# Turning softmax rows into columns: through DRAM and 32×32 blocks on VectorE in place of TensorE transposes

## The chip, the cores and the metric

The kernel runs on one core of a Trainium2 chip. The metric is the device time in microseconds (us) of one execution. Engines are named as the profile names them: PE (TensorE; PEld is its weight load), DVE (VectorE), ACT (ScalarE), POOL (GpSimd) and SP (SyncE, which here only issues DMAs). Every execution works on the same inputs.

## The reference

A graph convolution on 1250 nodes of 1024 features is followed by a transformer layer over the same 1250 tokens. Only the layer's attention is touched by the change. It has 16 heads of width 64, and its value and output projections are mixtures of 8 experts with a gate of two.

```python
q = _rope(jnp.einsum('bsd,hdp->bhsp', x, Wq))
k = _rope(jnp.einsum('bsd,hdp->bhsp', x, Wk))
gv = _gate(x, Wsel_v)                 # sigmoid, the two largest of 8 kept
v = jnp.einsum('bsd,bhse,hedp->bhsp', x, gv, Wv)
att = jax.nn.softmax(jnp.einsum('bhsp,bhtp->bhst', q, k) / np.sqrt(P), axis=-1)
o = jnp.einsum('bhst,bhtp->bhsp', att, v)
go = _gate(x, Wsel_o)
return jnp.einsum('bhsp,bhse,hepd->bsd', o, go, Wo)
```

All of it is float32. Ahead of it stand a layer norm, the graph convolution and another layer norm; behind it a residual with layer norms and a feed-forward block.

## The kernel before

**Arithmetic.** A float32 operand is split into a rounded part `hi` and the rest `lo`, both of a type that PE multiplies at full rate. `dot` makes three matmuls of each product: hi·hi, hi·lo and lo·hi. ACT makes `hi` (a copy that rounds), and DVE or POOL makes `lo` (a subtraction).

**Stages.** (1) The graph convolution, in tiles of KT = 125 nodes. (2) `queries_keys`: for each head, queries and keys together (128 rows: 64 of queries, 64 of keys) over the 1250 tokens in three pieces of columns, with the gates' work between them. (3) `values` and `attention`, interleaved. (4) `outputs`, with the last of the attention. (5) `feed_forward`.

**Stage 2.** A head's hi and lo parts are collected in the tiles `qk_hi` and `qk_lo` (two buffers each, so a head waits until the tiles of the head before the last one are free). When the head's third piece is done, SP issues six writes to DRAM (`kq_d`, lines 594 and 596): two of the key rows and four of the query rows, each of 64 rows of 1250 floats. The weights of later heads (line 123) are loaded by the same SP queue.

**Stage 3.** `values` makes, for each head and tile of 125 tokens, a product of eight steps of depth with 512 columns (8 experts × 64), in four value steps of six matmuls each; then DVE multiplies by the gate (`ve`, line 717) and adds the experts (`v`, line 720). There are 40 value steps a head and 640 in all.

`attention` works on chunks of 256 query rows, five a head and 80 in all, each in two halves of 128 rows. `softmax` (line 622) loads q and, once a head, k by POOL's queue; PE makes the scores in three PSUM banks (line 634); DVE takes the rows' maximum (`most`, line 637); ACT makes the exponentials and their sums (line 642); DVE multiplies the rows by 1/sum (line 647). Then the rows have to become columns, since PE sums over partitions. `split` (line 650) does that for two tiles of 125 keys at a time, five times a chunk: four transposes by PE (line 655) into a PSUM bank, `att_hi` by ACT (line 657), `att_lo` by DVE (line 659). `product` (line 664) multiplies them with the values, four matmuls of 256 columns, into the bank `po`. After the last tile the sum goes to `o_d` in DRAM by SP.

**Order.** PE's instructions stand in the order in which the program writes them (`manual_schedule`). In stage 3 this is a fixed interleaving of generators: of eight value steps seven are followed by one event of the attention, in the order of this line:

```python
for event in (0, "k", "k", 1, "k", "k", "k"):
```

0 and 1 are the halves' scores of the next chunk, and a "k" is one `split` and one `product` that was split two events earlier. The order of the other engines and of the queues is set by a scheduler when the program is built. Each engine, and SP, works through its own order and waits where it must: a later instruction does not pass an earlier one.

**Stage 4.** `outputs` takes for every pair of heads and half of the experts five column blocks of 250 tokens. SP loads `oc` (the attention's result, line 736) and `gb` (the gate, spread over partitions, line 741); DVE multiplies them (line 745); ACT and DVE split into `go_hi` and `go_lo` (lines 748 and 750); PE multiplies by the output weights, and DVE adds into `acc` (line 765).

**PSUM.** In stages 3 and 4 there are, of eight banks, two for values or outputs (`mm`), two for the transposes (`tr`), three for scores and one for `po`.

Of the kernel before, what the change touches and what calls it, by code (L numbers as in the profile page):

```python
# [11 lines left out]
F32 = mybir.dt.float32  # L12
# [10 lines left out]
N = 1250  # L23
# [13 lines left out]
CUT = NZ * KT  # L37
# [33 lines left out]
def gnn_ffn_kernel(  # L71
# [31 lines left out]
    o_d = [dram.tile([P, N], F32, name=f"o_d{j}") for j in range(NP)]  # L103
    g_d = dram.tile([P, N], F32, name="g_d")
# [61 lines left out]
    def transposed(hi, lo, c0, y, psum_tile):  # L166

        for half in range(2):
            p = psum_tile([P, 4, KT])
            for k in range(4):  # L170
                d0 = (4 * half + k) * P
                nc.tensor.transpose(p[:, k, :], y[:, d0 : d0 + P], ident[:KT, :KT])
            to = (slice(None), slice(4 * half, 4 * half + 4), slice(c0, c0 + KT))
            nc.scalar.copy(hi[to], p)
            nc.vector.tensor_tensor(lo[to], p, hi[to].bitcast(F32), ALU.subtract)
# [8 lines left out]
    with ExitStack() as gctx:  # L184
# [16 lines left out]
        with ExitStack() as bctx:  # L201
# [3 lines left out]
            with tc.tile_pool(name="ring1t", bufs=6) as r1:  # L205
                ring += [r1] * 6

                def prepare(t):
# [10 lines left out]
                    transposed(yh, yl, 0, y[:KT], lambda shape: ps.tile(shape, F32, name="tr2", bufs=2))  # L219
# [274 lines left out]
        zT = [[zpool.tile([P, ND, CUT], F32R, name=f"zT0{k}") for k in range(2)]]  # L494
        for t in range(2, NT):
            new = sums([t])
            if t - 2 < NZ:
                transposed(zT[0][0], zT[0][1], KT * (t - 2), zs.pop(0)[:KT], side_bank)
                zs += new
# [5 lines left out]
    def z_of(t, d):  # L505

        k = t if t < NZ else t - NZ
        return [part[:, d, KT * k : KT * (k + 1)] for part in zT[t >= NZ]]

    def rest_of_z():  # L510

        for t in range(NZ, NT):
            z = raws[0].tile([P, D], F32, name="w_raw")[:KT]
            move(z, z_d[t])
            transposed(zT[1][0], zT[1][1], KT * (t - NZ), z, side_bank)
# [3 lines left out]
    def gates(wpool, tmp):  # L519
# [5 lines left out]
        wide = [KT, 2 * H, NX]  # L525
        order = first_wins[:KT, None, :].to_broadcast(wide)

        def pick(chosen, v, m):

            nc.vector.tensor_reduce(m, v, AX.X, ALU.max)  # L530
# [5 lines left out]
        for t in range(NT):  # L536
            p = side_bank([KT, 2 * P])
# [3 lines left out]
            s, a, b, c = (tmp.tile([KT, 2 * H, NX], F32, name=k) for k in ("s", "a", "b", "chosen"))  # L541
            m = tmp.tile([KT, 2 * H], F32, name="m")
# [5 lines left out]
            nc.vector.tensor_tensor(gate_v[:KT, t, :].rearrange("p (h e) -> p h e", h=H), s[:, :H, :], c[:, :H, :],  # L548
                                    ALU.mult)
            nc.vector.tensor_tensor(a[:, H:, :], s[:, H:, :], c[:, H:, :], ALU.mult)  # L550
            pg = psums[-1].tile([P, KT], F32, name="po", bufs=1)
            nc.tensor.transpose(pg, a[:, H:, :].rearrange("p h e -> p (h e)"), ident[:KT, :KT])
            nc.scalar.copy(gT[:, KT * t : KT * (t + 1)], pg)
# [4 lines left out]
    def queries_keys(tab, work):  # L558
# [9 lines left out]
        chunks = [(0, 0, CUT), (1, 0, 376), (1, 376, N - CUT - 376)]  # L568
# [3 lines left out]
        for h, k in pieces:  # L572
# [19 lines left out]
            if k == 2:  # L592
                for j, part in enumerate((hi.bitcast(F32), lo.bitcast(F32))):
                    nc.sync.dma_start(kq_d[h][HD * j : HD * (j + 1), 0, :], part[HD:])
# [13 lines left out]
    with tc.tile_pool(name="qktab", bufs=1) as tab, tc.tile_pool(name="qkwork", bufs=2) as work, \  # L608
            tc.tile_pool(name="gatet", bufs=2) as tmp:
        turns, rest = queries_keys(tab, work), rest_of_z()  # L610
        interleave(islice(turns, 2), rest, 1, 1 / 3)
        interleave(turns, gates(tab, tmp), 1, 3)

# [3 lines left out]
    def attention(pool):  # L617


        keys, made = {}, {}  # L620

        def softmax(h, c, i):
# [5 lines left out]
            q = pool.tile([P, 2, P], F32R, name="q", bufs=4)  # L628
# [9 lines left out]
            p = pool.tile([P, N], F32, name="p", bufs=5)  # L638
            parts = pool.tile([P, 3], F32, name="parts", bufs=4)
            for k, k0 in enumerate(starts):  # L640
                n = KW if k == 2 else KW - 2
                nc.scalar.activation(p[:, k0 : k0 + n], s[:, k, :n], AF.Exp, bias=most,  # L642
                                     accum_out=parts[:, k : k + 1])
            total = pool.tile([P, 1], F32, name="total", bufs=4)
            nc.vector.tensor_reduce(total, parts, AX.X, ALU.add)
            nc.vector.reciprocal(total, total)
            nc.vector.tensor_scalar_mul(p, p, total)
            made.setdefault((h, c), []).append(p)

        def split(h, c, k):  # L650

            t = side_bank([KT, 2, QW])
            for j in range(2):
                for i, p in enumerate(made[h, c]):
                    nc.tensor.transpose(t[:, j, P * i : P * (i + 1)], p[:, KT * (k + j) : KT * (k + j + 1)], ident)  # L655
            hi = pool.tile([KT, 2, QW], F32R, name="att_hi", bufs=3)
            nc.scalar.copy(hi, t)  # L657
            lo = pool.tile([KT, 2, QW], F32R, name="att_lo", bufs=3)
            nc.vector.tensor_tensor(lo, t, hi.bitcast(F32), ALU.subtract)  # L659
            return hi, lo  # L660

        sums = {}

        def product(h, c, k, parts):
            if k == 0:
                sums[h, c] = psums[-1].tile([P, QW], F32, name="po", bufs=1)
            po = sums[h, c]
            for j in range(2):
                for part in parts:
                    nc.tensor.matmul(po, lhsT=v_of[h][:, k + j, :], rhs=part[:, j, :],  # L670
                                     start=(k + j == 0 and part is parts[0]),
                                     stop=(k + j == NT - 1 and part is parts[1]))
            if k + 2 < NT:
                return
            o = pool.tile([HD, QW], F32, name="o", bufs=2)
            nc.scalar.copy(o, po[HD:])
# [250 lines left out]
```

## Time and profile before

| what | value |
|---|---|
| median of 3 runs | 3134.45 us (3130.17 to 3136.78) |
| profiled execution, its own time | 3137.92 us |
| its span, first to last instruction | 3136.1 us |
| mean granted PE clock | 0.985 |
| PE busy | 3023.9 us (96%) |
| DVE, ACT, POOL busy | 62%, 35%, 22% |
| moved by DMA | 254.86 MB, mean 81 GB/s |

| stage | from, to (us from the span's start) | PE busy in it | DMA share |
|---|---|---|---|
| queries, keys, gates | 314 to 593 | 262.43 | 0.58 |
| values and attention | 593 to 2015 | 1416.31 | 0.21 |
| outputs | 2026 to 2997 | 940.65 | 0.36 |

How it is read. Busy time is the time in which an engine has an instruction under way. Matmuls are pipelined, so the spacing of their starts, not their duration, is what one costs PE. The DMA share is the mean busy share of the core's 16 DMA engines. In the groups, what stands behind the second bar is the idle time of the engine just before the group's instructions and what ended it. A profile shows one execution; the span and the device time of that execution differ by 1.8 us, and that execution took 3.5 us more than the median.

### The profile page before, as it was taken

What the parts mean: (1) busy time and instruction counts of PE and PEld (TensorE: products, weight loads), DVE (VectorE), ACT (ScalarE), POOL (GpSimd) and SP (SyncE); (2) the same over time, 40 slices, a digit from 0 to 9 for tenths busy, and PEclk for the clock granted to TensorE, in tenths of its full rate; (3) what the DMA queues carried; (4) which work ended last, traced back from release to release, by engine and by line L of the source; (5) the groups of instructions that cost most, each with busy time, mean ns of one, the idle gap of its engine ahead of it and who ended that gap; (6) DMA issues with size and microseconds to landing.
All of it is one profiled execution on the core that took longest, in us unless ns stands there. A gap on an engine that the chain in (4) does not pass through costs nothing. (4 is left out here: it accounts for less than half of the span.)

```text
span 3136.1 us, 41143 instructions
## 1 busy us (share of the span) xinstructions
PE 3023.9 (96%) x15618; PEld 2554.4 (81%) x15618; DVE 1957.2 (62%) x3477; ACT 1098.1 (35%) x2472; POOL 702.2 (22%) x570
## 2 busy tenths in 40 slices
PE   6989899999999999999999999899999999999998
PEld 5777889888888888888888888787777777777787
DVE  7965687566666666666666666664444444444685
ACT  5762323234444444444444444431112112111222
POOL 2000334322222122222212222202112112112223
PEclk9999999999999999999999999999999999999999
DMA  3116555612221121222112122434333333333212
GB/s 111 60 41 190 167 142 160 167 43 52 54 55 37 42 52 47 54 55 53 43 39 53 46 54 54 102 94 123 106 85 98 96 85 103 90 82 109 75 41 92
DMA packets 151825, 254.86 MB, mean 81 GB/s; under 512 B 14521, under 2 KB 111801, under 8 KB 151458
## 3 DMA queue, kind: packets, MB, share of 16 engines
q1 hardware_dynamic: 103934, 210.68, 23.9%
q0 software_dynamic: 45824, 31.22, 5.2%
q10 hardware_dynamic: 1860, 10.24, 1.1%
q8 instruction: 124, 2.03, 0.3%
q14 instruction: 83, 0.68, 0.1%
HBM read 200.25 MB, written 56.96 MB: 82 GB/s over the span
## 5 line engine op out<-in xcount | busy, mean ns | idle before, releaser
L129 POOL TENSOR_TENSOR w_lo<-w_raw,w_hi 128x1024 fp32r<-128x1024 f32 x148 | 372.3, 2525 | 1078.0 <-ACT w_hi L127 1069.6
L141 PE MATMUL mm<-w_hi,go_lo 128*125 128x512 f32 x1280 | 507.6, 399 | 24.6 <-DVE go_lo L750 24.5
L139 PE MATMUL mm<-w_hi,go_hi 128*125 128x512 f32 x1280 | 509.5, 398 | 8.8 <-ACT go_hi L748 7.9
L139 PE MATMUL mm<-w_hi,zT 128*125 128x512 f32 x1280 | 508.4, 397 | 4.6 <-ACT raw L584 4.6
L140 PE MATMUL mm<-w_lo,go_hi 128*125 128x512 f32 x1280 | 509.9, 398 | 0.0
L140 PE MATMUL mm<-w_lo,zT 128*125 128x512 f32 x1280 | 507.1, 396 | 0.1
L141 PE MATMUL mm<-w_hi,zT 128*125 128x512 f32 x1280 | 507.1, 396 | 0.0
L642 ACT ACTIVATE p<-s,most 128x416 f32<-128x416 f32 (+1 forms) x480 | 286.0, 605 | 332.8 <-DVE most L637 329.2
L765 DVE TENSOR_TENSOR acc<-acc,mm 125x512 f32<-125x512 f32 x320 | 217.4, 683 | 163.1 <-PE mm L141 163.1
L659 DVE TENSOR_TENSOR att_lo<-tr,att_hi 125x512 fp32r<-125x512 f32 x400 | 262.6, 685 | 88.7 <-ACT att_hi L657 88.6
L141 PEld LDWEIGHTS mm<-w_hi,go_lo 128*125 128x125 f32 x1280 | 239.9, 187 | 93.6 <-DVE go_lo L750 33.7
L748 ACT CAST go_hi<-gb 128x500 fp32r<-128x500 f32 x160 | 98.2, 614 | 602.2 <-PE mm L140 600.6
L657 ACT CAST att_hi<-tr 125x512 fp32r<-125x512 f32 x400 | 235.1, 589 | 179.0 <-PE tr L655 176.0
L139 PEld LDWEIGHTS mm<-w_hi,go_hi 128*125 128x125 f32 x1280 | 239.9, 187 | 68.3 <-ACT go_hi L748 8.2
L745 DVE TENSOR_TENSOR gb<-gb,oc 128x500 f32<-128x500 f32 x160 | 103.8, 690 | 303.0 <-DMA gb<-g_d 301.8
L141 PEld LDWEIGHTS mm<-w_hi,zT 128*125 128x125 f32 x1280 | 238.3, 186 | 60.5
L140 PEld LDWEIGHTS mm<-w_lo,go_hi 128*125 128x125 f32 x1280 | 239.7, 187 | 58.4
L637 DVE TENSOR_REDUCE most<-s 128x1 f32<-128x1254 f32 x160 | 234.2, 1464 | 81.0 <-PE s L634 80.6
L655 PEld LDWEIGHTS tr<-ident,p 128*125 128x125 f32 x1600 | 234.9, 187 | 53.6 <-DVE att_lo L659 18.6
L139 PEld LDWEIGHTS mm<-w_hi,zT 128*125 128x125 f32 x1280 | 239.1, 187 | 41.0 <-ACT raw L584 4.9
L140 PEld LDWEIGHTS mm<-w_lo,zT 128*125 128x125 f32 x1280 | 239.6, 187 | 36.5 <-POOL w_lo L129 0.4
L655 PE MATMUL tr<-ident,p 128*125 128x128 f32 x1600 | 242.0, 274 | 10.2 <-DVE att_lo L659 8.1
(201 smaller groups left out, 5166.6 us busy)
## 6 DMA issues: line engine op xcount, KB each, us to landing
gb<-g_d SPq DMA_DIRECT2D x160, 250.0 KB
w_raw<-in_wv SPq DMA_DIRECT2D x64, 512.0 KB
w_raw<-in_wo SPq DMA_DIRECT2D x64, 512.0 KB
q<-kq_d POOLq DMA_DIRECT2D x160, 128.0 KB, 2.6
kq_d<-qk_hi SPq DMA_DIRECT2D x48, 312.5 KB
kq_d<-qk_lo SPq DMA_DIRECT2D x48, 312.5 KB
k<-kq_d POOLq DMA_DIRECT2D x16, 625.0 KB, 4.4
oc<-o_d SPq DMA_DIRECT2D x80, 125.0 KB
```

Source lines behind the costliest of these rows:

```text
L129: (lo_engine or nc.gpsimd).tensor_tensor(lo, raw, hi.bitcast(F32), ALU.subtract)
L139: nc.tensor.matmul(p, lhsT=lhs[0], rhs=rhs[0], start=start, stop=False)
L140: nc.tensor.matmul(p, lhsT=lhs[0], rhs=rhs[1], start=False, stop=False)
L141: nc.tensor.matmul(p, lhsT=lhs[1], rhs=rhs[0], start=False, stop=stop)
L637: nc.vector.tensor_reduce(most, s[:, :, :KW], AX.XY, ALU.max, negate=True)
L642: nc.scalar.activation(p[:, k0 : k0 + n], s[:, k, :n], AF.Exp, bias=most, accum_out=parts[:, k : k + 1])
L655: nc.tensor.transpose(t[:, j, P * i : P * (i + 1)], p[:, KT * (k + j) : KT * (k + j + 1)], ident)
L657: nc.scalar.copy(hi, t)
L659: nc.vector.tensor_tensor(lo, t, hi.bitcast(F32), ALU.subtract)
L745: nc.vector.tensor_tensor(gb[:, :, mine], gb[:, :, mine], o[:, None, mine].to_broadcast([P, 4, KT]), ALU.mult)
L748: copied = nc.scalar.copy(hi, gb[:, :, mine])
L765: nc.vector.tensor_tensor(acc[t][:, cols], acc[t][:, cols], p, ALU.add)
```

## The change

`split` no longer uses PE. After the exponentials, the rows of a half go to DRAM unscaled, and come back in another order; DVE transposes the 32×32 blocks of what came back, and the blocks then stand as columns. For that the keys' order is changed ahead: `kq_d` holds the key rows in blocks of 32, permuted, so that the scores come out in an order in which block transposes give whole tiles of 128 keys. The products, `ACT`'s `hi` and `DVE`'s `lo` read the turned tile in SBUF, in two halves a chunk. The result's columns are put in order when `po` is read.

The factor 1/sum goes to DRAM (`r_d`, one float a row) and is applied to `oc` in `outputs`. Values and gates use tiles of 128 tokens (nine of 128, one of 98), so that a tile fits four blocks. The transposes' two PSUM banks go to `mm`, which has four. PE's order in stage 3 becomes: scores of half 0, second half of the product of the chunk before the last, scores of half 1, first half of the product of the last chunk, with two value steps behind each.

```diff
-CUT = NZ * KT
+CUT = NZ * P
+NB = 32
+NA = P // NB
+KA = NT * NB
...
+    r_d = [dram.tile([2, N], F32, name=f"r_d{j}") for j in range(NP)]
+    p_d = [dram.tile([NA, P, KA], F32, name=f"p_d{k}") for k in range(4)]
...
@@ queries_keys
-                    nc.sync.dma_start(kq_d[h][HD * j : HD * (j + 1), 0, :], part[HD:])
+                    to, n, last = kq_d[h][HD * j : HD * (j + 1), 0, :], (NT - 1) * NB, (NT - 1) * P
+                    for a in range(NA):
+                        nc.sync.dma_start(to[:, KA * a : KA * a + n].rearrange("p (b j) -> p b j", j=NB),
+                                          part[HD:, :last].rearrange("p (b a j) -> p b a j", a=NA, j=NB)[:, :, a, :])
+                        nc.sync.dma_start(to[:, KA * a + n : min(KA * (a + 1), N)],
+                                          part[HD:, last + NB * a : min(last + NB * (a + 1), N)])
@@ attention, softmax
-            q = pool.tile([P, 2, P], F32R, name="q", bufs=4)
+            q = pool.tile([P, 2, P], F32R, name="q", bufs=2)
...
-            p = pool.tile([P, N], F32, name="p", bufs=5)
+            p = pool.tile([P, N], F32, name="p", bufs=2)
...
+            d = p_d[(2 * n + i) % len(p_d)]
+            whole = KA * (NA - 1)
+            nc.sync.dma_start(d[: NA - 1].rearrange("a r k -> r a k"),
+                              p[:, :whole].rearrange("r (a k) -> r a k", a=NA - 1))
+            nc.sync.dma_start(d[NA - 1, :, : N - whole], p[:, whole:])
+            t = turned[n, i] = pool.tile([P, NA * KA], F32, name="turned", bufs=3)
+            nc.sync.dma_start(t, d.rearrange("a (i A) k -> (a i) (A k)", A=NA))
+            nc.vector.transpose(t, t)
...
-            nc.vector.tensor_scalar_mul(p, p, total)
+            new = max(QW * c - c0, 0)
+            nc.sync.dma_start(r_d[h // 2][h % 2, c0 + new : c0 + P][:, None], total[new:])
@@ attention, split
-            t = side_bank([KT, 2, QW])
-            for j in range(2):
-                for i, p in enumerate(made[h, c]):
-                    nc.tensor.transpose(t[:, j, P * i : P * (i + 1)], p[:, KT * (k + j) : KT * (k + j + 1)], ident)
-            hi = pool.tile([KT, 2, QW], F32R, name="att_hi", bufs=3)
-            nc.scalar.copy(hi, t)
-            lo = pool.tile([KT, 2, QW], F32R, name="att_lo", bufs=3)
-            nc.vector.tensor_tensor(lo, t, hi.bitcast(F32), ALU.subtract)
+            hi, lo = (pool.tile([P, 2 * NA, KA // 2], F32R, name=k, bufs=2) for k in ("att_hi", "att_lo"))
+            for i in range(2):
+                x = turned[n, i].rearrange("p (A k) -> p A k", A=NA)[:, :, KA // 2 * half : KA // 2 * (half + 1)]
+                mine = slice(NA * i, NA * (i + 1))
+                nc.scalar.copy(hi[:, mine], x)
+                nc.vector.tensor_tensor(lo[:, mine], x, hi[:, mine].bitcast(F32), ALU.subtract)
@@ attention, product
+            for b in range(NT // 2):
+                t = NT // 2 * half + b
+                rows = min(P, N - P * t)
+                for part in parts:
+                    nc.tensor.matmul(po, lhsT=v_of[h][:rows, t, :], rhs=part[:rows, :, NB * b : NB * (b + 1)],
+                                     start=(t == 0 and part is parts[0]), stop=(t == NT - 1 and part is parts[1]))
...
@@ attention, order
+        for d in p_d:
+            nc.sync.dma_start(d[NA - 1, :, N - KA * (NA - 1) :], zeros)
+        for n in range(len(chunks) + 2):
+            if n < len(chunks):
+                softmax(n, 0)
+            yield
+            if n > 1:
+                product(n - 2, 1)
+            yield
+            if n < len(chunks):
+                softmax(n, 1)
+            yield
+            if 0 < n <= len(chunks):
+                for half in range(2):
+                    split(n - 1, half)
+                product(n - 1, 0)
             yield
@@ outputs
-                    o = pool.tile([P, QB], F32, name="oc", bufs=2)
+                    o = pool.tile([P, QB], F32, name="oc", bufs=1)
                     nc.sync.dma_start(o, o_d[j][:, QB * c : QB * (c + 1)])
+                    r = pool.tile([P, QB], F32, name="r", bufs=1)
+                    for h2 in range(2):
+                        nc.sync.dma_start(r[HD * h2 : HD * (h2 + 1)],
+                                          r_d[j][h2 : h2 + 1, QB * c : QB * (c + 1)].to_broadcast([HD, QB]))
+                    nc.vector.tensor_tensor(o, o, r, ALU.mult)
@@ stages 3 and 4
-    banks[:] = [2, 2]
+    banks[:] = [4, 0]
...
-                if k >= per_head - per_chunk and k % per_chunk < 7:
-                    if k >= per_head or k % per_chunk in (0, 3):
-                        next(heads)
+                if k >= per_head - 16 and k % 2 == 0:
+                    next(heads)
...
-        made = sum(1 for _ in zip(heads, main))
+        made = 0
+        for _ in heads:
+            made += len(list(islice(main, 2)))
```

## The prediction

> **What bounds the kernel now.** I read the page first, then a table of stages, then TensorE's (PE's), VectorE's (DVE's) and SyncE's (SP's) timelines. Times are us unless said otherwise.
>
> ```profile
> PE 3023.9 (96%) x15618; PEld 2554.4 (81%) x15618; DVE 1957.2 (62%) x3477; ACT 1098.1 (35%) x2472; POOL 702.2 (22%) x570
> ```
>
> PE is busy almost throughout. Whether that holds where the change works, the stages tell (columns: stretch, length, busy time of PE, PEld, DVE, ACT, POOL, clock, DMA share, GB/s):
>
> ```profile
> 314.00:593.00 279.00, 262.43 (x1452) 243.74 (x1450) 207.73 (x396) 85.33 (x150) 103.60 (x69) 0.96 0.58 163
> 593.00:2015.00 1422.00, 1416.31 (x7738) 1227.83 (x7739) 936.63 (x1382) 611.88 (x1587) 358.15 (x395) 1.00 0.21 51
> 2026.00:2997.00 971.00, 940.65 (x4097) 749.64 (x4097) 489.96 (x738) 192.04 (x310) 171.58 (x68) 0.99 0.36 95
> ```
>
> First queries and keys: PE busy, but the DMA engines already at 0.58. Then values with attention: PE 1416 of 1422, DMA 0.21, DVE 66%. Then outputs. A PE instruction saved in the second stage is time saved, as long as nothing else becomes late there.
>
> ```profile
> 1500.47 0.60 PE L655 MATMUL tr<-ident,p 128*125 128x128 f32 x4
> 1500.82 0.36 PE L670 MATMUL po<-att_hi,v 125*128 125x256 f32 x1
> 1501.02 0.28 PE L670 MATMUL po<-att_lo,v 125*128 125x256 f32 x1
> 1501.14 0.28 PE L670 MATMUL po<-att_hi,v 125*128 125x256 f32 x1
> 1501.26 0.28 PE L670 MATMUL po<-att_lo,v 125*128 125x256 f32 x1
> 1501.38 0.40 PE L139 MATMUL mm<-w_hi,zT 128*125 128x512 f32 x1
> ```
>
> Start to start, four transposes hold PE for 0.35, the product after them 0.20 instead of 0.12. The durations (0.60 here, mean 274 ns in the groups) overlap and must not be summed.
>
> ```profile
> 1499.28 1.47 DVE L637 TENSOR_REDUCE most<-s 128x1 f32<-128x1254 f32 x1 [0.36 <-PE s L634]
> ...
> 1517.32 1.47 DVE L637 TENSOR_REDUCE most<-s 128x1 f32<-128x1254 f32 x1 [0.38 <-PE s L634]
> ```
>
> The same place of the cycle, one chunk (256 query rows) later: a chunk takes 18.04. DVE waits for PE, not the reverse.
>
> ```profile
> 571.43 0.45 SPq L594 DMA_DIRECT2D kq_d<-qk_hi  x1
> 571.92 1.75 SPq L596 DMA_DIRECT2D kq_d<-qk_hi  x2
> 573.77 1.08 SPq L594 DMA_DIRECT2D kq_d<-qk_lo  x1
> 574.89 2.88 SPq L596 DMA_DIRECT2D kq_d<-qk_lo  x2
> ...
> 584.27 0.45 SPq L594 DMA_DIRECT2D kq_d<-qk_hi  x1
> ```
>
> A head's six writes and one load fill the DMA engines for some 10 of 12.8 us here (8.05 and 2.2 by the packet records). From the first head's writes (366.5) to the last's (597.1), gates included, a head takes 15.4.
>
> **TensorE's saving.** 20 transposes a chunk go: 5 groups × (0.35 + 0.08) = 2.15. A chunk on PE alone would take 18.04 − 2.15 = 15.9. Over 80 chunks that is 172, the most this change can gain. The Trainium skill ("VectorE: DVE Perf Modes", The three transpose paths) speaks against the change: it gives 390 ns for a 128×128 transpose on TensorE and 311 ns on VectorE, which does only 32×32 blocks, and advises TensorE where PSUM will do. Taken as PE's price, 390 ns would make the gain 1600 × 0.39 = 624, an estimate; the row's 0.0875 a transpose decides, and the gain is a quarter of that.
>
> **The new loop through DRAM.** In the changed program's order each block transpose stands on DVE directly behind the maximum of the next half-chunk, and behind it wait a value tile's gating (whose PSUM bank PE needs), the lo halves and, last, the maximum after next. So from one maximum to the next but one, which is a whole chunk, this chain must close:
> - Exponentials: three L642 rows run from 1500.78 to 1502.66: 1.9.
> - Write of p, 640 KB in 512 pieces of 1280 and 1160 B. SP to first packet: 0.95 to 1.35 in this trace (a 512 KB weight; a 256-piece `gb`); I take 1.1. Packets: 2.5 at the rate of the 625 KB `g_d` write (2.44), 3.7 at that of the 1000 B pieces of `gb` (512 in 2.84); between the sizes I take 3.1, and 0.2 to the landing: 4.4.
> - SP wakes (0.1) and reads 655 KB back in rows of 5120 B: 0.95 + 2.5 + 0.2 = 3.65, scaled from the weights (512 KB: 3.1 from issue to landing). DVE wakes: 0.1.
> - The block transpose, 1280 elements. Nearest is the stream shuffle: 723 ns for 500, 586 ns for 376, so 1.1 ns an element: 1.58, or 1.5 start to start.
> - Behind it, in the slower of two alternating orders: total 0.19, reciprocal 0.20, three lo halves 0.8 each (scaled from `w_lo` on DVE, 1444 ns for 1024 elements, to 0.9, less 0.1 of overlap), o 0.34, ve 0.8, v 1.05, maximum 1.47: 6.45.
>
> Sum: 1.9 + 4.4 + 3.75 + 0.1 + 1.5 + 6.45 = 18.1, against 18.04 now and 15.9 on PE. The saving goes into this loop. DVE's work alone is no bound: 12.0 a chunk now, less 3.0 (five lo from PSUM) and 1.6 (p times 1/sum), plus 3.0 and 3.2, is 13.6; it is the wait in its order that costs.
>
> The loop shares the DMA engines with itself and others: twice 5.6 of packets a chunk, two q loads of 0.85, four fifths of a weight at 2.2, and keys: some 16 of 18. I add 0.65 for contention (0 to 2.2, one weight ahead of p): 18.75, so +0.7 × 77 chunks (of 640 value steps, 24 pass before attention starts) = **+54**. Bounds: 16.9 (packets of the write in 2.5, lo at 0.6 start to start as now from PSUM), −88; 20.9 (write in 3.7, contention 2.2), +220.
>
> **Weights behind the loop.** SP's order puts a head's four value weights between these writes and reads, and each waits for POOL to free a raw buffer; p's next write is queued behind that wait. Today SP only has o behind it. 0 to 4 × 2.2 a head; I take 2 × 15 = **+30** (0 to +130).
>
> **Keys in blocks of 32.** A head's key rows go out in 16 DMAs instead of 2, as 5120 pieces of mostly 128 B instead of 128 of 5000 B. Packet records give the pitch on each of 16 engines: 512 B 53 ns, 1000 B 89, 4096 B 275, 5000 B 335, a line of about 26 ns + 0.062 a byte. No 128 B data packet is in the trace: below, 13 ns (53/4); above, 89 ns; the line says 34, I take 40 since these are writes and 14 more DMAs a head are issued. 5120/16 × 40 ns = 12.8, with the four row writes (5.4) and a weight (2.2) 20.4 a head against 15.4 now. The tiles `qk_hi` and `qk_lo` have two buffers and come free when these writes land, so PE follows: 5.0 × 15 = **+75** (0 at 11.8 a head; +310 at 36.1). The Trainium skill ("DMA: Bandwidth & Descriptors", Specifications) says that under 512 B the engine does a read-modify-write; no run here shows that, and it would push towards the upper end.
>
> **The rest.** Outputs: 80 multiplications of 128×250 (about 0.35), 160 small broadcast loads, and `oc` in one buffer instead of two. The next load then waits for a multiplication, with the weights' loads queued behind it on SP; two go_hi buffers leave PE 11 us of cover. **+10** (0 to +35; 28 if the multiplications lie open). Tiles of 128 tokens keep the number of matmuls and columns; exponentials and k loads stay; q has two buffers instead of four, and half a chunk (9) to hide its 2.6 from issue to landing; r_d's 4-byte writes (20 000 packets) and the zero fill lie beside the loop; four value banks instead of two gain nothing where PE is at 1416 of 1422. These I cost at nothing.
>
> **Sum.** The profiled execution's own time is 3137.9: + 54 + 30 + 75 + 10 = 3306.9. The median shown lies 3.5 lower: **3303**.
>
> **Rivals.**
> 1. Forecast, both prices paid: 3303, own range 3180 to 3450. Chance 0.62.
> 2. Faster: the loop closes under PE's time. It needs write and read at 262 GB/s with no contention, and key pieces near 20 ns. A chunk at 16.9 is −88; with keys +10 and outputs +10 the median is about 3066. For it: DMA share 0.21 today. Against: 18.1 from middle rows. It decides below 18.04 a chunk, if the keys hide too. Chance 0.17, of which 0.02 ends level.
> 3. Much slower: the DMA engines become the bound. Chunk 20.5 (+189) and packets at 70 ns (30 a head, +219), weights +60, outputs +10: about 3612. For it: 16 of 18 us taken. Against: loads back to back reach 266 GB/s here. Chance 0.21.
> That the change does not do what it says I exclude: the built program has none of the 1600 L655 instructions.
>
> **How the numbers follow.** About 0.2% is what a measurement can tell from no change. Faster 0.15, same 0.03, slower 0.82. Range 3110 to 3560: it leaves out most of the second case and the upper part of the third.
>
> **What would show it.** Right: no transposes of p on PE; PE below 90% in the values; DVE idle before the block transpose, ended by the DMA of `turned`; chunk pitch 18 to 20; block transpose near 1.6; the query-key stage 60 to 100 longer with DMA share above 0.8, PE waiting there behind ACT's copy. Wrong: chunk pitch near 16 (the loop hides), a query-key stage as long as before (small pieces are cheap), or a loss in the outputs.

## The result, and the profile after

The changed kernel takes **3953.9 us** (median of 4 runs, 3944.5 to 3971.1) against 3135.5: ratio 1.262, 95% interval 1.257 to 1.267. The profiled execution has 3947.1, with a span of 3945.3. The forecast was 3303 with a range to 3560: right in sign, wrong in size by 650. Times are us.

The stages of the changed kernel (stretch, length, busy time of PE, PEld, DVE, ACT, POOL, clock, DMA share, GB/s):

```profile
324.00:675.00 351.00, 257.58 (x1412) 237.15 (x1411) 194.95 (x389) 84.16 (x147) 100.04 (x68) 0.87 0.66 121
675.00:2757.00 2082.00, 1523.95 (x6272) 1233.92 (x6272) 988.56 (x1317) 623.71 (x1524) 340.09 (x395) 0.85 0.77 131
2784.00:3812.00 1028.00, 946.38 (x3988) 744.30 (x3988) 547.97 (x803) 185.43 (x289) 168.97 (x69) 0.97 0.43 107
```

From the first products of queries and keys (314 in both) the three stages end at 593, 2016 and 3002 before, at 675, 2757 and 3813 now. So the first lost 82, the values 659, the pause behind them and the outputs 70. In the values no compute engine is at its limit: PE 1524 of 2082 at a clock of 0.85, DVE 989. The DMA engines are at 0.77, and yet they move only 131 GB/s.

What DVE waits for (the group of the block transpose: busy time, mean ns of one, idle time before it and what ended it), and two of these instructions a chunk apart:

```profile
L677 DVE STREAM_TRANSPOSE turned<-turned 128x1280 f32<-128x1280 f32 x160 | 241.9, 1512 | 1022.4 <-DMA turned<-p_d 1022.4
```

```profile
1504.57 1.51 DVE L677 STREAM_TRANSPOSE turned<-turned 128x1280 f32<-128x1280 f32 x1 [6.76 <-DMA turned<-p_d]
...
1532.60 1.51 DVE L677 STREAM_TRANSPOSE turned<-turned 128x1280 f32<-128x1280 f32 x1 [7.83 <-DMA turned<-p_d]
```

One transpose takes 1.51, as forecast, but waits 6.4 for the read of `turned`. A chunk takes 27 (median over all chunks; 28.0 here) against 18.1. Why is the read late? SP's own queue shows what it issues:

```profile
1500.21 0.48 SPq L674 DMA_DIRECT2D p_d<-p  x1
1506.34 0.32 SPq L682 DMA_DIRECT2D r_d<-total  x1
1506.76 0.38 SPq L676 DMA_DIRECT2D turned<-p_d  x1
1512.83 0.37 SPq L672 DMA_DIRECT2D p_d<-p  x1
```

Right ahead of the read stands the write of the 128 factors 1/sum, L682. In the trace's completion records its 16 landings (one for each DMA engine) come from 3.9 to 7.9 after its issue, though it moves 512 bytes, and the last landing of the read behind it comes after 10.9. Over the run the median of the last landing is 8.1 for the write and 10.3 for a read directly behind it; the quickest tenth of all these reads land within 5.2. No instruction of the stage waits for that write itself. The forecast had put it at nothing.

### The profile page after: what moved, and what is told of

The parts are those of the page before. It is cut to its first block, busy times and chain, and to the rows that moved or that the text cites. A ratio compares the mean times of both kernels' runs of the same rounds, so it can differ in the third digit from the quotient of the medians.

```text
span 3945.3 us, 39836 instructions
## 1 busy us (share of the span) xinstructions
PE 3139.7 (80%) x14018; PEld 2552.6 (65%) x14018; DVE 2058.9 (52%) x3480; ACT 1103.5 (28%) x2394; POOL 676.1 (17%) x570
## 5 line engine op out<-in xcount | busy, mean ns | idle before, releaser
L677 DVE STREAM_TRANSPOSE turned<-turned 128x1280 f32<-128x1280 f32 x160 | 241.9, 1512 | 1022.4 <-DMA turned<-p_d 1022.4
L145 PE MATMUL mm<-w_hi,zT 128*128 128x512 f32 (+1 forms) x1280 | 565.8, 442 | 5.8 <-ACT raw L600 5.8
L146 PE MATMUL mm<-w_lo,zT 128*128 128x512 f32 (+1 forms) x1280 | 560.5, 438 | 0.0
L147 PE MATMUL mm<-w_hi,zT 128*128 128x512 f32 (+1 forms) x1280 | 551.2, 431 | 0.0
L145 PE MATMUL mm<-w_hi,go_hi 128*125 128x512 f32 x1280 | 513.5, 401 | 25.6 <-ACT go_hi L790 24.1
L704 PE MATMUL po<-att_hi,v 128*128 128x256 f32 (+1 forms) x800 | 247.5, 332 | 307.2 <-DVE o L713 123.5
L690 ACT CAST att_hi<-turned 128x640 fp32r<-128x640 f32 x320 | 224.3, 725 | 879.8 <-DVE total L679 726.5
L660 PE MATMUL s<-k,q 128*128 128x418 f32 x960 | 251.7, 404 | 216.0 <-ACT p L668 214.6
L145 PEld LDWEIGHTS mm<-w_hi,zT 128*128 128x128 f32 (+1 forms) x1280 | 279.6, 218 | 65.1 <-ACT raw L600 6.2
L147 PEld LDWEIGHTS mm<-w_hi,zT 128*128 128x128 f32 (+1 forms) x1280 | 270.9, 212 | 74.2
L146 PEld LDWEIGHTS mm<-w_lo,zT 128*128 128x128 f32 (+1 forms) x1280 | 274.3, 214 | 57.0
L704 PE MATMUL po<-att_lo,v 128*128 128x256 f32 (+1 forms) x800 | 250.4, 337 | 70.1 <-DVE att_lo L691 70.1
L145 PEld LDWEIGHTS mm<-w_hi,go_hi 128*125 128x125 f32 x1280 | 242.0, 189 | 87.7 <-ACT go_hi L790 26.6
L691 DVE TENSOR_TENSOR att_lo<-turned,att_hi 128x640 fp32r<-128x640 f32 x320 | 260.1, 831 | 27.4 <-ACT att_hi L690 26.9
```

Of the source, the lines that this page charges most:

```text
L145: nc.tensor.matmul(p, lhsT=lhs[0], rhs=rhs[0], start=start, stop=False)
L146: nc.tensor.matmul(p, lhsT=lhs[0], rhs=rhs[1], start=False, stop=False)
L147: nc.tensor.matmul(p, lhsT=lhs[1], rhs=rhs[0], start=False, stop=stop)
L660: nc.tensor.matmul(s[:, k, :KW], lhsT=q[:, part, :], rhs=keys[h][:, k0 : k0 + KW], start=(part == 0), stop=(part == 1))
L677: nc.vector.transpose(t, t)
L690: nc.scalar.copy(hi[:, mine], x)
```

## The experiments

**Theory R**: the 160 writes of `r_d`, 128 pieces of 4 bytes each, hold up the reads and writes of p. **Rival B**: p's own traffic fills the DMA engines. **Rival C**: a read directly behind the write of the same rows is slow by itself. Chunk times below go from a maximum of the scores to the same one a chunk later; where "median" stands, it is that of single chunks. Landings are from the completion records: the last of a DMA, counted from its issue.

### Without the writes: e1_no_r

```
-            new = max(QW * c - c0, 0)
-            nc.sync.dma_start(r_d[h // 2][h % 2, c0 + new : c0 + P][:, None], total[new:])
...
+        for j in range(NP):
+            nc.sync.dma_start(r_d[j], cos[HD // 2 : HD // 2 + 2, :])
```

> The changed kernel without the 160 writes of r_d in the loop; r_d is set once to rows of `cos`, so the outputs lack the factor 1/sum. Sums and reciprocals are still computed. Theory R: these writes (128 pieces of 4 B, some 8 us to land) hold up the read of `turned` that stands behind them in SP's queue (10.3 us from issue to landing, 4.5 to 5.4 at its quickest). Without them the read lands in 4 to 5, a half-chunk shortens by 4 to 5 us, a chunk takes 18.5 to 19.5 instead of 27 to 28, the values lose some 600 us, the whole about 3350 (3290 to 3430). DMA share in the values falls from 0.77 to below 0.5. Rival B (the 16 engines are taken up by p's writes and reads themselves) and rival C (a read directly behind the write of the same rows is slow by itself): the chunk stays at 25 or more, the whole above 3800, the read stays near 10.

This kernel leaves out the factor 1/sum. Measured: 3172.5, ratio to the kernel before 1.013 (1.011 to 1.014). The 160 writes cost **781** of the 818 lost. Chunk 16.8 (median; mean 17.4). The transposes' wait and the values' stage of this kernel:

```profile
L677 DVE STREAM_TRANSPOSE turned<-turned 128x1280 f32<-128x1280 f32 x160 | 241.7, 1511 | 263.8 <-DMA turned<-p_d 263.7
```

```profile
672.00:2028.00 1356.00, 1287.04 (x6265) 1066.71 (x6263) 992.45 (x1313) 620.51 (x1523) 335.71 (x394) 0.99 0.66 200
```

The wait falls from 1022 to 264. The same traffic of p now runs at 200 GB/s, and the stage is 66 *shorter* than before the change (1356 against 1422). Rivals B and C fall: write and read of p are quick (2.8 from issue to landing for each write, 3.9 for a read behind them). Theory R holds, but the gain was expected too small: the whole is below the 3290 to 3430 expected and the chunk below 18.5 to 19.5. The DMA share stays at 0.66 instead of falling below 0.5; the same bytes go through in two thirds of the time.

### Through another queue: e2_r_pool

```
-            nc.sync.dma_start(r_d[h // 2][h % 2, c0 + new : c0 + P][:, None], total[new:])
+            nc.gpsimd.dma_start(r_d[h // 2][h % 2, c0 + new : c0 + P][:, None], total[new:])
```

> The changed kernel with the write of r_d issued from POOL's queue instead of SP's; nothing else differs. Theory R1 (the 4 B pieces stand ahead of the read in the same queue): the read lands in 4 to 5 and the chunk falls to 18.5 to 20, the whole to about 3350 to 3450; the loads of q and of keys, which go through POOL's queue, then land later instead (q 6.5 now, 10 or more expected). Theory R2 (the pieces take up the 16 engines, whatever queue they come from): the read stays above 8, the chunk above 24, the whole above 3750. Rivals B and C: no change, 3900 to 3960.

Measured: 3785.5 (1.208; 1.205 to 1.210), chunk 24.1 (median). Only 168 of the 781 are won, so it isn't the order in SP's queue alone. A read directly behind p's writes now lands in 3.8, but the writes themselves take 6.9 and 7.5 instead of 2.8: here the other transfers under way while the pieces land are late too. The loads of q show it from POOL's queue (last column: median from issue to landing). First the changed kernel, then e1_no_r, then e2_r_pool:

```profile
q<-kq_d POOLq DMA_DIRECT2D x160, 128.0 KB, 6.5
```

```profile
q<-kq_d POOLq DMA_DIRECT2D x160, 128.0 KB, 2.8
```

```profile
q<-kq_d POOLq DMA_DIRECT2D x160, 128.0 KB, 8.9
```

By the chunk and the whole, theory R2 of the expectation holds; that a read lands in 3.8 again is R1's part.

### The writes alone, in the kernel before: e11_before_r

```
             nc.vector.reciprocal(total, total)
+            nc.sync.dma_start(r_d[h // 2][h % 2, c0 : c0 + P][:, None], total)
```

> The kernel before with one thing added: the 160 writes of 1/sum to r_d, 128 pieces of 4 B each, on SP's queue, with nothing that reads them. It prices the term that the prediction set at nothing where no read of p stands behind it. Theory H (they cost by holding up what is behind them; here that is o's writes, weights and q, all with buffers ahead): 3135 to 3200. Rival (they cost wherever they are): 3400 or more.

Measured: 3257.9 (1.040; 1.038 to 1.043), between the two expectations: **+125**. The values of this kernel (in the kernel before, the same stage has a DMA share of 0.21 at 51 GB/s):

```profile
593.00:2130.00 1537.00, 1458.95 (x7771) 1250.76 (x7770) 964.29 (x1392) 614.33 (x1600) 359.37 (x397) 0.98 0.42 50
```

The rate is the same, the share of the engines twice as high. No p goes through DRAM here, and still the write lands after 7.8 and a weight directly behind it after 10.1 (weights issued more than 13 after the last such write: 3.6). Over five chunks, one takes 19.4 instead of 18.2. So some 8 us belong to the write itself. In the changed kernel the same writes cost 656 more; there a read that DVE waits for runs through the same engines twice a chunk.

### What makes them slow: e5_kinds, e6_sizes, e9_strides

Each kernel is e1_no_r with a dummy write a half-chunk whose form changes every four heads (`rk2_d` has a row of 128 floats for each piece). Each ran once; what is compared are groups of heads in one execution:

```
+            if h < 4:
+                nc.sync.dma_start(rk1_d[one][:, None], total)
+            elif h < 8:
+                nc.sync.dma_start(rk2_d[one][:, :1], total)
+            elif h < 12:
...
+                nc.sync.dma_start(row.rearrange("o (p k) -> o p k", k=1), total)
+            else:
...
+                nc.vector.tensor_copy(block, total.to_broadcast([P, NB]))
+                nc.vector.transpose(block, block)
+                nc.sync.dma_start(rk1_d[one].rearrange("(b k) -> b k", k=NB),
+                                  block.rearrange("(b j) k -> b j k", j=NB)[:, 0, :])
```

> The kernel of e1_no_r (r_d constant, so the outputs lack 1/sum) with a dummy write of the 128 sums a half-chunk in four ways, by heads. Heads 0 to 3: 128 pieces of 4 B side by side, as r_d was; 4 to 7: 128 pieces of 4 B, each in a block of 512 B of its own; 8 to 11: 128 pieces of 4 B into one SBUF row instead of DRAM; 12 to 15: the sums turned on DVE by a 32x32 block transpose and written as 4 pieces of 128 B. Chunk of e1_no_r: 17.4; of the changed kernel: 26 to 27. Theory L (pieces that fall into one block of DRAM wait for each other): 26 in the first group, 17 to 19 in the second, 17 to 18 in the others. Theory S (each 4 B piece to DRAM costs its engine about 1 us, wherever it goes): 26 and 26, then 17 to 18 twice. Theory N (128 tiny pieces cost by their number, whatever the target): 26 in the first three, 17 to 18 in the last.

The four groups of heads in e5_kinds (columns as in the stages above):

```profile
708.00:1245.00 537.00, 390.51 (x1589) 318.65 (x1587) 249.26 (x335) 159.94 (x393) 87.67 (x101) 0.84 0.78 129
1245.00:1597.00 352.00, 327.16 (x1581) 270.60 (x1582) 254.65 (x340) 161.44 (x396) 85.98 (x100) 0.98 0.66 198
1597.00:1941.00 344.00, 325.79 (x1611) 269.93 (x1610) 255.89 (x342) 161.90 (x397) 86.66 (x100) 1.00 0.67 203
1941.00:2201.00 260.00, 244.39 (x1194) 202.30 (x1194) 200.42 (x318) 123.14 (x301) 68.98 (x76) 0.99 0.66 203
```

Twenty chunks in 537, 352 and 344, fifteen in 260: 26.9, 17.6, 17.2 and 17.3 a chunk. The first and second group send the same 128 pieces of 4 bytes from the same queue to DRAM; only the second keeps them 512 bytes apart, and it costs nothing that shows. Theory L holds; neither the number of the pieces nor their size by itself makes the cost. In the first group the packets of one write all start within 0.2 of each other and last 7 to 9 ns in the records, but the landings drag from 4.0 to 8.4 (medians of the first and the last); in the second they come between 1.2 and 1.4 in the quickest tenth.

```
+            wide = pool.tile([P, P], F32, name="wide", bufs=2)
+            nc.vector.tensor_copy(wide[:, :m], total.to_broadcast([P, m]))
+            nc.sync.dma_start(x_d[h // 4][2 * n + i - 40 * (h // 4)], wide[:, :m])   # m = 8, 16, 32, 128
```

> The kernel of e1_no_r (outputs without 1/sum) with a dummy write a half-chunk of 128 pieces, each piece beside the next: heads 0 to 3 32 B a piece, 4 to 7 64 B, 8 to 11 128 B, 12 to 15 512 B. Theory T (a write below some line of DRAM of 32 or 64 B is slow): 26 at and above nothing, that is 32 B pieces still 22 to 26, 64 B and larger 17.5 to 18.5. Theory 512 (any piece below 512 B is slow): 26 for 32, 64 and 128 B, 18 only for 512 B; the 128 B key pieces of the changed kernel speak against it. Theory L of e5_kinds (shared 512 B blocks): 32 to 128 B above 20 with the least at 128 B, 512 B 18.

e6_sizes: 17.4, 17.3, 17.3 and 17.7 a chunk for 32, 64, 128 and 512 bytes side by side, median landings 3.3 to 3.8. All three expectations put something above 20; none is. Pieces of 32 bytes that touch cost no more than larger ones. The next run changes the distance of 4-byte pieces.

```
+            nc.sync.dma_start(rs_d[h // 4][2 * n + i - 40 * (h // 4)][:, :1], total)   # rows of 2, 4, 8, 16 floats
```

> The kernel of e1_no_r (outputs without 1/sum) with a dummy write of 128 pieces of 4 B a half-chunk, whose starts lie apart by 8 B (heads 0 to 3), 16 B (4 to 7), 32 B (8 to 11) and 64 B (12 to 15). So far: 4 B apart, last landing 8.4 and chunk 26.9; 512 B apart, 2.4 and 17.6. Theory L (pieces of one line wait for each other): the wait halves with each step, landings some 5, 3, 2, 1.5 to 2.4, chunks about 22, 18.5, 17.5, 17.5; if the line is 32 B, 32 B apart is as quick as 64. Theory 512 (a whole block of 512 B is the line): the same fall, but 64 B apart still above 512 B apart by 0.3 or more. Rival (only pieces that touch are slow): all four at 17 to 18.

The groups of e9_strides, 4 bytes written every 8, 16, 32 and 64 bytes (the last over fifteen chunks):

```profile
705.00:1105.00 400.00, 345.26 (x1587) 280.62 (x1586) 252.24 (x336) 160.50 (x393) 87.95 (x101) 0.95 0.71 173
1105.00:1469.00 364.00, 328.95 (x1587) 267.47 (x1586) 254.44 (x341) 161.96 (x396) 86.74 (x100) 1.00 0.68 191
1469.00:1820.00 351.00, 326.52 (x1611) 269.67 (x1610) 254.70 (x341) 161.69 (x397) 86.75 (x100) 1.00 0.67 199
1820.00:2085.00 265.00, 244.81 (x1185) 201.65 (x1185) 195.06 (x257) 123.95 (x301) 67.63 (x75) 0.99 0.67 199
```

Put together (landing: last of the 16 after the issue, quickest tenth of 40 and median):

| distance of the pieces (bytes) | 4 | 8 | 16 | 32 | 64 | 512 |
|---|---|---|---|---|---|---|
| landing, quickest tenth | 7.7 | 3.8 | 2.0 | 1.4 | 1.4 | 1.4 |
| landing, median | 8.4 | 4.8 | 3.5 | 2.4 | 3.0 | 2.4 |
| chunk | 26.9 | 20.0 | 18.2 | 17.6 | 17.7 | 17.6 |

With 8, 4, 2 and 1 pieces in 32 bytes, the quickest landings' excess over 1.4 is 6.3, 2.4, 0.6 and 0, that is 0.6 to 0.9 for each further piece. From 32 bytes on it is gone, as theory L has it for a line of 32 bytes; the first step falls further than expected (20.0 a chunk and not 22). What these runs show is the cost by distance. That the pieces of one line wait for one another is the reading that fits it; no record shows the waiting itself.

### Keys written plainly: e3_keys_view

```
-                    for a in range(NA):
-                        nc.sync.dma_start(to[:, KA * a : KA * a + n].rearrange("p (b j) -> p b j", j=NB),
...
+                    nc.sync.dma_start(kq_d[h][HD * j : HD * (j + 1), 0, :], part[HD:])
...
+            in_blocks = keys[h].rearrange("p (b a j) -> p a b j", a=NA, j=NB)
+                    nc.tensor.matmul(s[:, k, :KA], lhsT=q[:, part, :], rhs=in_blocks[:, k],
```

> The changed kernel with the key rows written plainly again, 2 DMAs a head instead of 16; the order of the keys in blocks of 32 is made by a strided view of the moving operand of the score matmuls, in four banks of 320 columns (8 matmuls and 4 exponentials a half-chunk instead of 6 and 3). Theory: the query-key stage loses what it gained, 60 to 85 us, since the last three weights no longer stand behind the key writes of seven heads; the values keep their chunk of 27 to 28, as they wait for DMAs and not for PE or ACT: about 3870 (3840 to 3910). Rival: the strided reads make PE slow or the exponentials' extra 0.2 us a half lies in the loop: +30 to +60 in the values, the whole 3900 to 3950.

The fourth bank of scores is taken from the values, which have three instead of four. Measured: 3888.3 (1.243; 1.239 to 1.246), as its theory had it. The last `qk_hi` is copied at 595.7, against 678.7 in the changed kernel and 596.5 before: the key writes cost 82, and a strided view gives them back; 66 are left in the whole time. The values, bound by the DMAs, keep 26.6 a chunk (median).

### What the key writes cost with: e7_keys16, e10_keys_act, e13_wqk_pool

In the changed kernel SP issues one key write after the other, 20 a head with the queries' rows:

```profile
565.24 0.60 SPq L613 DMA_DIRECT2D kq_d<-qk_hi  x1
565.89 0.72 SPq L615 DMA_DIRECT2D kq_d<-qk_hi  x1
566.84 0.60 SPq L613 DMA_DIRECT2D kq_d<-qk_hi  x1
```

That is 17 to 18 a head, and the last three query-key weights stand behind six heads of it (505.6 to 618.1). PE waits for them (group of the stage, 314 to 676):

```profile
L145 PE MATMUL mm<-zT,w_hi 128*128 128x512 f32 (+2 forms) x384 | 139.2, 363 | 76.8 <-ACT w_hi L133 70.8 <-ACT raw L600 6.0
```

```
-                    for a in range(NA): ...                       # e7_keys16
+                    for a in range(2 * NA):
+                        some = slice(157 * a, min(157 * (a + 1), N))
+                        nc.sync.dma_start(to[:, some], part[HD:, some])

-                        nc.sync.dma_start(to[:, KA * a ...        # e10_keys_act, both block writes
+                        nc.scalar.dma_start(to[:, KA * a ...

-                heads[h] = (weights(wqk[h]), ...                  # e13_wqk_pool
+                heads[h] = (weights(wqk[h], queue=nc.gpsimd), ...
```

> The changed kernel with the 16 key writes a head cut as plain column ranges (16 DMAs of 64 pieces of 628 B) in place of 128 B blocks; the keys stand in plain order, so the order of p's columns in the product is left wrong. It tells what the 72 us of the query-key stage are (351 against 279 before, 275 with two plain DMAs a half). Theory I (SP needs 0.6 us for each of 20 DMAs a head and the last weights stand behind them): the stage stays 345 to 360. Theory P (128 B pieces are slow in the engines): it falls to 275 to 295. The values keep 26 to 28 a chunk.

> The changed kernel with the 16 block writes of the keys of each head issued from ACT's queue instead of SP's; the row writes and the weights stay on SP. Query-key stage so far: 279 before, 351 changed, about 300 with 16 plain DMAs. Theory Q (the last weights stand behind key writes in SP's queue): 285 to 310, PE's wait for w_hi falls from 71 to below 30; ACT is busier by its issues. Theory P (the 128 B pieces fill the engines): 345 or more. If ACT's issues hold up the copies that PE waits for: above 360. The values stay at 26 to 28 a chunk.

> The changed kernel with the loads of the query-key weights issued from POOL's queue instead of SP's, so that they no longer stand behind the key writes; the key writes are those of the changed kernel, 16 DMAs of 128 B pieces a head. Query-key stage: 279 before, 351 changed, some 300 with 16 plain DMAs; with the key writes on ACT's queue 16 issues a head held up ACT's copies and it took longer, which told nothing of the pieces. Theory Q (the stage is lost by the order in SP's queue): PE's wait for w_hi there, 71, falls below 20 and the stage to 280 to 310. Theory P (the pieces or the number of DMAs hold the engines or SP, so that `qk_hi` and `qk_lo` come free too late): 335 to 360, PE waits for ACT's copies into `raw` or for `qk_hi` instead. The values stay at 26 to 28 a chunk, the whole 3890 to 3960.

Each of the three ran once. The last `qk_hi` comes at 620.9 in e7_keys16 (whole 3867.5; it leaves the keys in plain order), at 736.0 in e10_keys_act (3984.0) and at 617.5 in e13_wqk_pool (3919.3). e7_keys16 lies between its two theories: from the first product of queries and keys to the first of the values it takes 307, where the changed kernel has 360. e10_keys_act is the third of its expectations: PE waits 112 up to its first value products for ACT's copies into `raw`, since these now stand behind the issues on ACT, and a head takes 23.6; it says nothing on the pieces. e13_wqk_pool decides, and it has the very pieces of the changed kernel:

```profile
L145 PE MATMUL mm<-zT,w_hi 128*128 128x370 f32 (+2 forms) x381 | 137.2, 361 | 2.9 <-ACT raw L600 2.1 <-ACT zT L181 0.7 <-ACT w_hi L133 0.2
```

```profile
600.00:656.00 56.00, 3.82 (x8) 2.71 (x9) 9.08 (x21) 6.40 (x10) 12.06 (x12) 0.53 0.79 154
```

PE's wait for `w_hi` falls from 71 to 0.2 and the queries and keys are ready 61 earlier (4 of them already at the stage's first product). But PE is idle from 598 to 650 (second line), for the first value weights stand on SP directly behind the last head's writes:

```profile
641.30 1.08 SPq L618 DMA_DIRECT2D kq_d<-qk_lo  x2
642.68 2.20 SPq L129 DMA_DIRECT2D w_raw<-in_wv  x2
```

So of the 61 some 34 are left in the whole time. To the first value product the stage still takes 339, a number of theory P, but by none of the waits that theory P names. Counted from the stage's first product to the last `qk_hi`, 57 of the 82 go once the query-key weights no longer stand behind the key writes on SP, with the pieces as they are: it is the order in SP's queue, with the time that 20 issues a head take, that costs most. In e7_keys16, with as many DMAs of plain pieces, 53 go; SP takes some 16 a head there instead of 17 to 18, and issues the last three weights at 564.1 to 573.2 instead of 618.1 to 628.3. How much of these 53 is the pieces, and how much the order, these runs don't tell.

### 1/sum in p: e4_mul_p

```
...
+            nc.vector.tensor_scalar_mul(p, p, total)
...
-            nc.sync.dma_start(r_d[h // 2][h % 2, c0 + new : c0 + P][:, None], total[new:])
...
-                    nc.vector.tensor_tensor(o, o, r, ALU.mult)
```

> The changed kernel with 1/sum multiplied into p before it is written, as the kernel before had it; no r_d, no r in the outputs, two buffers for `oc`. Theory R: no 4 B writes, so the read lands in 4 to 5; but the multiplication (about 0.9) and the two small operations stand on DVE ahead of the write and are queued behind the last block transpose: chunk 20 to 23, the whole 3400 to 3600, outputs some 30 to 50 shorter than with the changed kernel. Rivals B and C: chunk 28 or more, the whole 3950 to 4100.

Measured: 3305.4 (1.056; 1.054 to 1.057), 95 below the lowest expected; chunk 18.3 (median), 19.5 (mean), outputs 964 where e1_no_r has 998. Better than the changed kernel by 649, though the multiplication of p stands ahead of its write: another way to see that the small write is what costs. It is slower than e1_no_r by 133.

### Both costs taken out: e8_rows and e12_r_early

e8_rows is e3_keys_view with the 128 factors turned on DVE and written as four rows of 128 bytes:

```
+            block = pool.tile([P, NB], F32, name="block", bufs=2)
+            nc.vector.tensor_copy(block, total.to_broadcast([P, NB]))
+            nc.vector.transpose(block, block)
+            nc.sync.dma_start(r_d[h // 2][h % 2, c0 : c0 + P].rearrange("(b k) -> b k", k=NB),
+                              block.rearrange("(b j) k -> b j k", j=NB)[:, 0, :])
```

> The changed kernel with its two costs taken out and all of the computation in: the keys' order by a strided view (as e3_keys_view) and r_d written as 4 pieces of 128 B after a 32x32 block transpose of the sums on DVE. From e1_no_r (3172): query-key stage 358 to 277, two small DVE operations (0.1 to 0.2) and a fourth exponential (0.2) a half-chunk, hidden or in the loop: 0 to +50. Expected 3110 (3085 to 3150), chunk 17 to 18, a little below the kernel before (3133). If the small pieces cost as 4 B ones do: above 3300.

Measured: **3080.6** (5 runs, 3079.2 to 3082.3), ratio 0.983 (0.980 to 0.985): 1.7% faster than the kernel before, and a little under the range expected.

```profile
PE 2882.8 (94%) x14338; PEld 2379.9 (77%) x14338; DVE 2110.1 (69%) x3800; ACT 1141.1 (37%) x2714; POOL 693.8 (23%) x586
```

```profile
314.00:593.00 279.00, 261.30 (x1455) 241.28 (x1454) 209.79 (x401) 87.02 (x153) 105.21 (x70) 0.97 0.58 165
593.00:1930.00 1337.00, 1281.84 (x6580) 1069.29 (x6578) 1023.12 (x1621) 658.56 (x1829) 352.35 (x410) 1.00 0.66 203
1944.00:2945.00 1001.00, 941.08 (x4001) 741.84 (x4002) 557.20 (x821) 188.04 (x301) 169.25 (x70) 0.98 0.41 111
```

Queries and keys as before (279), the values 85 shorter, outputs 25 longer than before (1001 against 976), the pause ahead of them 5. PE is busy 1282 of 1337 in the values, so with PE's work as it is at most 55 more could be had there.

```
...
+                r_of[n] = pool.tile([HD, QW], F32, name="r", bufs=1)                 # e12_r_early
+                nc.sync.dma_start(r_of[n], r_d[h // 2][h % 2 : h % 2 + 1, first : first + QW].to_broadcast([HD, QW]))
...
+            nc.vector.tensor_tensor(o, o, r_of.pop(n), ALU.mult)
```

> e8_rows with 1/sum applied to o in the attention (one load of r for 64 partitions and one multiplication of 64x256, about 0.4, a chunk) instead of in the outputs, and two buffers for `oc` again. The outputs stage falls from 1001 to about 968, as e4_mul_p had it (964); the values stay or gain 0 to 15. Expected 3055 (3040 to 3080) against 3081.

Measured: 3083.1 (0.984; 0.982 to 0.986): no gain over e8_rows, where 3040 to 3080 had been expected. The outputs fall to 970 as expected (first product at 1984.7, last at 2954.3), but the values end at 1972 instead of 1930. One more load and multiplication a chunk in the loop gives back what the outputs win.

## Why the prediction was wrong, point by point

- **The factors' write**: the failed step. "r_d's 4-byte writes (20 000 packets) and the zero fill lie beside the loop", costed at nothing. Measured: +781 in the changed kernel, whose read and writes of p run through the same engines, and +125 in the kernel before. "Beside the loop" is right as far as nothing in the loop waits for this write. What is missing is what else must pass the same engines, and how long 128 pieces in 512 bytes of DRAM take to land: 8.1. The forecast looked at what stands in SP's order for the weights, and not for this write, which stands there directly ahead of the read in 67 of 160 cases.
- **The loop**: mechanism right, size too high. Forecast 18.75 a chunk; without the factors' write the median is 16.8 (mean 17.4). In that kernel's trace two terms come out smaller. The write of p: 4.4 forecast, 3.2 from the first issue to the last landing. What DVE does behind a block transpose up to the end of the maximum after next: 6.45 forecast, 4.8 and 5.7 in the two orders. The exponentials (1.9), the read (3.75 forecast, 3.9 measured directly behind the writes) and the block transpose (1.5, 1.51) stand. From the end of a maximum to the start of its block transpose, which holds exponentials, write and read, 10.8 and 9.6 pass in these two orders, where the forecast adds up 10.15: of what the write saves, at most half arrives. So the values gain 66 to 85 where +54 was forecast; −88 was the bound.
- **TensorE's saving**: no transposes of p are left, and PE's busy time in the values falls by 129 (e1_no_r) to 134 (e8_rows), against a cap of 172. But its idle time there grows from 6 to 69 and 55, and so the stage gets only 66 and 85 shorter.
- **Weights behind the loop**: +30 forecast, not measured by itself. e1_no_r's mean chunk is 0.7 above its median, some 50 over 80 chunks, but part of that is the last head's, which no value steps accompany. No run here gives this term; it stays open.
- **Keys in blocks**: +75 forecast, +82 measured, for another reason. The 128-byte packets took 13 ns (median; the forecast's lowest bound) and not 40. Forecast was that `qk_hi` and `qk_lo` come free too late; in fact SP issues 20 DMAs a head, most at 0.6, and weights stand behind them; e13_wqk_pool gives 57 of the 82 back by the order alone. The DMA share was 0.66, not above 0.8, and PE waited for `w_hi` and not for ACT's copy of queries and keys: both signs named in the forecast failed. The right number was luck.
- **Outputs**: +10 forecast (0 to 35). In e1_no_r the outputs are 21 longer than before and the pause ahead of them 5; e4_mul_p, without the multiplication by r, is at 964. So the multiplications lie open, the 28 that the forecast named as that case. In the changed kernel pause and outputs together are 70 longer; the other 44 go with the factors' write.
- **The rivals**: the third (the DMA engines become the bound, 3612) names the right engines for the wrong reason: they show a share of 0.77, but at 131 GB/s, where e1_no_r moves 200 at 0.66. The second (faster, 3066: the loop closes under PE's time and the keys hide) is what e8_rows does, 3080.6, once the costs of the small DMAs and of SP's order are out.
- **Signs**: chunk pitch 18 to 20 had been named; 27 shows at once that a term was missing. The other signs of being right (PE below 90% in the values, DVE idle until the DMA of `turned`) came true, but would have done so with any slow read.

## What to carry to other kernels

Price every DMA of a moved step by its pieces and by where they land, even if nobody waits for it; it shares the engines with transfers that somebody does wait for. One value a partition was cheaper turned on chip (two small DVE operations, 0.2 each) and written as rows. Where DMAs are cut into many, count them against the issuing queue's pace, and look at which loads stand behind them.

## What the runs showed of the hardware

- Writes of 4 bytes were slow where several fell into 32 bytes of DRAM: 7.7 to land with eight there, 1.4 with one. The packet records of the write don't show it (7 to 9 ns each); the landings do, and so do packets of the next transfer (5120 bytes in the changed kernel's values: 196 ns median, but a mean of 0.69 us against 0.24 in e1_no_r, and up to 8.2 us). The Trainium skill ("DMA: Bandwidth & Descriptors", Specifications) sets a line at 512 bytes, under which a read-modify-write is done; in e6_sizes 32, 64, 128 and 512 bytes side by side cost the same (17.3 to 17.7 a chunk), and in e5_kinds 4 bytes in a block of their own cost no more. The line that these runs show is at 32 bytes, and only for several pieces in one.
- A high DMA share isn't bandwidth: 0.78 at 129 GB/s with the slow write, 0.66 at 198 without, for the same p.
- SP, and ACT in e10_keys_act, took 0.6 to 0.7 for the issue of most such key writes, some of them 1.6 to 1.7; twenty issues are the larger part of a head's 17 to 18.
- The granted clock was lower where PE waited more: 0.85 in the changed kernel's values (PE busy 73%), 0.95 in those of e4_mul_p (88%), 0.99 and 1.00 in those of e1_no_r and e8_rows (95% and 96%). With it goes PE's busy time of 1524 in the changed kernel, though it has less to do than before (1416).
